# Cross attention over 64 head groups: the value products of two groups in one run, and value loads at another place in the queue

## The chip, the cores and the metric

The kernel runs on one core of one Trainium2 chip. The metric is the device time of one execution in microseconds. Engines: TensorE (PE, its weight loads PEld), VectorE (DVE), ScalarE (ACT), GpSimd (POOL), and SyncE (SP), which here only issues transfers (DMAs).

## The reference, cut to what matters

`x` and the context have shape (8, 256, 1024), all f32, and there are 32 heads of 32. Keys and values are both the context itself.

```python
xn = (x - mean(x)) * rsqrt(var(x) + 1e-5) * gamma + beta      # over the last axis
Q, K, V = split_heads(xn @ Wq.T), split_heads(ctx), split_heads(ctx)
scores = where(mask, einsum('bhsd,bhtd->bhst', Q, K) * 32 ** -0.5, -inf)
attn = einsum('bhst,bhtd->bhsd', softmax(scores), V)           # heads joined again
out = x + attn @ Wout.T
```

## The kernel before, in words

The attention is cut into 64 quads: quad n is batch n // 8 and the four heads of group n % 8. One iteration n of the main loop (a slot) holds, for every engine, what it does in that slot; each engine runs its instructions in the order in which the program writes them. In slot n:

- TensorE computes the scores of quad n + 1 (`scores`, L486: 32*128 tiles, four score banks), then the value products of quad n - 2 (`values`, L629: 64*32 tiles, 32 matmuls in the program, 64 in the trace), then full 128*128 work: query products for later quads (L345, L447) and output products for the batch before (`product_steps`, L715). Both projections are computed with seven products of halves in place of eight, from sums of halves which POOL makes (`sum_x`, `sum_at`, `sum_wq`, `sum_wo`). The table STEPS says how many output steps stand before the values, behind them and at the end of each slot.
- `softmax(n + 1)` spreads over DVE (maximum and mask, L522; reciprocal, L533; 32x32 transposes of probabilities into pT, L541), ACT (exponentials, L526; `aside`, L547, which copies half of pT to pc; `copy_at`, L642, which evicts finished value products from PSUM into the buffers at; `copy_q` and others) and POOL (normalization, L535). `copy_at` for all finished quads stands behind the exponentials of the first head.
- SP then moves blocks of probabilities between partitions: two transfers pT<-pT (L607), other loads of the slot (the list `between`: keys every second slot, residual rows, weights kept in DRAM, and x for a later batch), two transfers pT<-pc (L611). The second two wait for the first two to land. The load of the values of quad n (`load_v`, L144), which waits for quad n - 2's products to be done with the buffer, is issued in slot n ahead of the moves of quad n + 1 (list `ahead`). At the end of a slot follow moves of normalized x (`move_x`, L332, six of them in some slots), weights to keep (`keep_wq`), and stores of the output (L758).

Buffers: pT has three, v two, at three, the value products' PSUM pool `ps_v` two banks, the scores' pool four. So the products of quad n - 2 must be done before softmax(n + 1) can write pT, and a value load waits for the products two quads before.

`sum_at` makes the sums of the attention output. S1 = S2 + A11 is made on POOL at the end of the sixth slot of a block (i = 5), in the place of S2, and reads the first half buffer of at; i = (n - 8) % 8. Ahead of the main loop stand 32 transposes of the identity (`busy`, L120), which keep TensorE at work until x has been loaded and normalized.

Of the kernel before, what the change touches and what calls it, by code (L numbers as in the profile page):

```python
# [46 lines left out]
F32 = mybir.dt.float32  # L47
# [4 lines left out]
P = 128  # L52
# [7 lines left out]
def xattn_kernel(  # L60
# [12 lines left out]
    B, S, D = x.shape  # L73
# [3 lines left out]
    NQ = NC  # L77
    NH = P // HD
    NS = S // P
    NT = T // P  # L80
    NO = D // 512
    K = 32
# [4 lines left out]
    N = B * NQ  # L87
# [16 lines left out]
    ps_v = ctx.enter_context(tc.tile_pool(name="ps_v", bufs=2, space=PS))  # L104
# [11 lines left out]


    busy = ps_s.tile([P, P], F32, tag="sc", name="busy")
    for _ in range(32):
        nc.tensor.transpose(busy, ident, ident)  # L120


# [2 lines left out]
    def load_x(b, s, h=None):  # L125

        if b not in xs:
            xs[b] = xp.tile([P, NS, D], F32, tag="x", name=f"x_{b}")
        cols = ds(0, D) if h is None else ts(h, 512)
        nc.sync.dma_start(xs[b][:, s, cols], x[b, ts(s, P), cols])  # L130
# [9 lines left out]
    def load_v(n):  # L140

        b, g = divmod(n, NQ)
        vs[n] = vp.tile([P, NI, P], F32, tag="v", name=f"v_{n}")
        nc.sync.dma_start(  # L144
            vs[n],
            kv[b, g // 2, :, ds(2 * T + n % 2 * NI * P, NI * P)].rearrange("p (i v) -> p i v", i=NI),
        )
# [164 lines left out]
    def blocks_x(b, s):  # L312

        if s == 0:
            xes[b] = xp.tile([P, NA, NC, NS, K], F32, tag="x", name=f"xe_{b}")
        nc.vector.transpose(
            xes[b][:, :, :, s, :],
            xs[b][:, s, :].rearrange("p (c q k) -> p q c k", c=NC, q=NA),
        )

    def move_x(b, part):

        if 0 in part:
            tile_ = lnp.tile([P, NC * (S + 1)], F32, tag="xnT", name=f"xnT_{b}")
            xnT = tile_[:, : NC * S].rearrange(
                "p (a c s k) -> p a c s k", a=NA, c=NC, s=NS
            )
            to_move[b] = xnT
            xnTs[b] = lambda c: xnT[:, :, c, :, :]
        for i in part:  # L330
            a, q = i % NA, (i + i // NA) % NA
            nc.sync.dma_start(to_move[b][ts(q, K), a], xes[b][ts(a, K), q])  # L332
# [138 lines left out]
    mbs, scs, pTs, pvs, ats, pos = {}, {}, {}, {}, {}, {}  # L471
# [146 lines left out]
            tail()  # L618
        yield

    def values(n):
        pvs[n] = [
            ps_v.tile([P, 2, NS, K], F32, tag="pv", name=f"pv_{n}_{r}") for r in range(2)
        ]
        pT = pTs.pop(n)
        for i in range(NI):
            for j in range(NH):
                for r in range(2):
                    nc.tensor.matmul(  # L629
                        pvs[n][r][j * HD : (j + 1) * HD],  # L630
                        vs[n][ts(r, 2 * K), i, ts(j, HD)],
                        pT[ts(r, 2 * K), :, i, j, :, :],
                        start=(i == 0), stop=(i == NI - 1),
                    )
# [160 lines left out]
    for n in range(N):  # L795
# [12 lines left out]
    loads, stats, norms, trans, moves, biases, masks = (  # L808
        {n: [] for n in range(N)} for _ in range(7)
    )  # L810
    for b in range(1, B):
# [3 lines left out]
        elif b == 2:  # L815
            when = dict(
                loads=(0, 1), stats=(2, 3), norms=(3, 3), trans=(4, 5),
                moves=tuple(5 + (i + 2) // 6 for i in range(16)),
            )
        else:  # L820
            when = dict(
                loads=(first - 12, first - 11) if b == SPLIT else (first - 13, first - 12),
# [84 lines left out]
    for b in range(B - 1):  # L907
        done, ends = 0, b == B - 2
        for i, counts in enumerate(steps_of(b)):
            n = NQ * (b + 1) + i  # L910
# [10 lines left out]
    def project_steps(n, place):  # L921
        for one in steps.get((n, place), ()):
            product_steps(*one)


    for n in range(N):
        b, i = divmod(n - NQ, NQ)
        new_q = new_qs[n]
        between = []
        if n % 2 == 0 and n + 4 < N:  # L930
            between.append(partial(load_k, n + 4))
        ahead = [partial(load_v, n)] if n > 1 else []
        between += rings[n]
        if b >= 0:
            if b == B - 2 and i - 1 in (5, 6):
                between.append(partial(send, b, *ENDS_TO[i - 1]))
            if i < 4:
                between.append(partial(load_res, b, *((0, 0), (0, 1), (1, 1), (1, 0))[i]))
        between += [partial(load_x, *args) for args in loads[n]]
        between += [partial(load_mask, one) for one in masks[n]]  # L940
        if n in (3, 4):
            between.append(partial(load_wo, B21, n - 3))
        if n == N - 4:
            again = xp.tile([P, NS, D], F32, tag="x", name="x_again")
            for s in range(NS):
                between.append(partial(nc.sync.dma_start, again[:, s, :], x[B - 1, ts(s, P), :]))

        if n + 1 < N:
            scores(n + 1)
        project_steps(n, 0)  # L950
        hooks, now, behind = {}, [], []
        for what, one, *args in evacuations[n]:
            if one == B - 2:
                now.append(partial(what, one, *args))
            else:
                place = 0 if i in (3, 4, 6) or i < 3 and what is not add_p1 else "soon" if i == 2 else 1
                if one not in P1_ASIDE and i in (1, 2):
                    place = "p1" if what is keep_p1 else "soon"
                hooks.setdefault(place, []).append(partial(what, one, *args))
        if n >= 2:  # L960
            values(n - 2)
        project_steps(n, 1)
        copies = [partial(copy_q, q) for q in new_q]
        if n in halves and n % 2 == 0:
            make_q(halves[n], second=True, chunks=range(NC // 2, NC))
            copies.insert(0, partial(copy_q, halves[n]))
        for q in new_q:
            make_q(q)
        if n in products:
            query_product(*products[n])  # L970
            copies.append(partial(copy_product, *products[n]))
        for one in now:
            one()
        fill = []
        if n < 2:
            transpose_x1(2 * n)
            transpose_x1(2 * n + 1)
            fill = [partial(copy_x1, 2 * n), partial(copy_x1, 2 * n + 1)]
        elif n <= NQ:
            fill = [partial(ln_stats, *args, parts=(i,)) for args in stats[n] for i in range(3)]  # L980
            fill += [partial(blocks_x, *args) for args in trans[n]]
        if n + 1 < N:
            softmax(n + 1, copies, ahead, between, hooks, fill)
        else:
            copy_at(n - 2)
            for load in ahead + between:
                load()
        if b >= 0 and i == 1:
            sum_at(b, "S2", *((slice(NK - 1, NK),) if b == B - 2 else ()))
        later = []  # L990
        if n > NQ:
            for args in stats[n]:
                ln_stats(*args, later=later)
        for args in norms[n]:
            ln_norm(*args, nc.scalar)
        if n > NQ:
            for args in trans[n]:
                blocks_x(*args)
        for args in moves[n]:
            move_x(*args)  # L1000
        for one in away[n]:
            one()
        for one in biases[n]:
            mask_bias(one)
        project_steps(n, 2)
        for one, slot in S3_SLOTS:
            if n == slot:
                sum_at(one, "S3")
        if b >= 0:
            for name in {2: ("S4",), 3 if b == B - 2 else 5: ("S1",)}.get(i, ()):  # L1010
                sum_at(b, name)
            if i == 0 and b == B - 2:
                sum_at(b, "S2", slice(0, NK - 1))
        for slot, name in ((n + 2, "S1"), (n + 2, "S2"), (n + 1, "S4"), (n - 1, "S3")):
            if slot in firsts:
                sum_x(firsts[slot], name)
        if b == B - 2:
            if i > 2:
                add_kept(b, i, *ENDS_TO[i])
        elif b >= 0 and i in (3, 4, 5):  # L1020
            add_p1(b, *{3: (0, 1), 4: (1, 1), 5: (1, 0)}[i])
        for one in later:
            one()
        if n in halves and n % 2:
            make_q(halves[n], second=True, chunks=range(NC // 2))
        if n == 0:
            nc.gpsimd.tensor_scalar(gs, gam, NEG_SCALE, 1.0, ALU.mult, ALU.mult)
        if n < NQ:
            fold(n)
        for one in sums[n]:  # L1030
            one()
        if N - NQ + 2 < n < N - 1:

            c = n - (N - NQ + 3)
            if c == 0:
                last = ps_q.tile([P, 512], F32, tag="pq", name="po_last")
            end_steps(last, "A11", B11, (c,), (0,))
# [100 lines left out]
```

## Time and profile before

| | |
|---|---|
| three timed runs | 576.61, 577.20, 577.48 us; median 577.2 |
| the profiled execution, from its first to its last instruction | 577.0 us |
| TensorE / weight loads / VectorE / ScalarE / GpSimd busy | 567.3 / 394.2 / 460.4 / 411.7 / 409.8 us |
| share of transfer time, SP's queue | 66.8% of 16 engines' span |
| HBM read / written | 60.04 / 10.49 MB |

The profiled execution is another one than the timed ones; its own time is told by its span alone, and that lies within them. In rows of a timeline the first number is the start in microseconds from the first instruction, the second the time from the first start to the last end of a run of like instructions, then come engine, line, operation, output <- input, form, count, and in brackets how long the engine had been idle before and what ended that. A matmul in the program is two in the trace. Matmuls are pipelined, so a run's stretch overlaps the start of the next.

### The profile page before, as it was taken

To read this page: it belongs to the slowest core of one execution; us is meant where nothing else is said; L and a number is where in the kernel's file an instruction comes from. 1 tells how busy PE (TensorE), PEld (TensorE's weight loads), DVE (VectorE), ACT (ScalarE), POOL (GpSimd) and SP (SyncE) were. 2 spreads that over 40 slices of the span, in tenths; PEclk is the share of its full clock that TensorE was granted. 3 is DMA by queue.
4 is the path that set the end of the run, shared out by engine and by line. 5 is a ranking of instruction groups with operands and counts; after the bars stand their busy time and mean duration, and the time that the engine had idled before them with its cause. 6 is when DMAs were issued, how large, how long until landed. Compare 5 with 4: busy or idle time off the path is not lost. (4 is left out here: it accounts for less than half of the span.)

```text
span 577.0 us, 20128 instructions
## 1 busy us (share of the span) xinstructions
PE 567.3 (98%) x7162; PEld 394.2 (68%) x7162; DVE 460.4 (80%) x1695; ACT 411.7 (71%) x1425; POOL 409.8 (71%) x677
## 2 busy tenths in 40 slices
PE   8999998999999999999999999999999999999997
PEld 8788784667667777677676677667766767755543
DVE  5888887788877879979888788988878878779823
ACT  4697886677667877688677867768767776769810
POOL 1778898889896896876568675676658657448770
PEclk9999999899999999999999999999999999999999
DMA  8974766656677777957678856687567864446751
GB/s 304 394 206 126 208 161 180 192 148 166 185 220 222 200 208 207 271 166 201 188 213 228 211 138 189 212 240 206 148 161 236 224 170 130 130 138 178 199 166 73
DMA packets 50100, 111.69 MB, mean 194 GB/s; under 512 B 9424, under 2 KB 10192, under 8 KB 50000
## 3 DMA queue, kind: packets, MB, share of 16 engines
q1 hardware_dynamic: 49712, 110.40, 66.8%
q8 instruction: 57, 0.93, 0.7%
q14 instruction: 43, 0.35, 0.2%
q10 hardware_dynamic: 288, 0.01, 0.0%
HBM read 60.04 MB, written 10.49 MB: 122 GB/s over the span
## 5 line engine op out<-in xcount | busy, mean ns | idle before, releaser
L535 POOL TENSOR_SCALAR e<-e,rden 128x256 f32<-128x256 f32 x512 | 236.0, 478 | 116.9 <-DVE rden L533 114.4
L526 ACT ACTIVATE e<-e,mn 128x256 f32<-128x256 f32 x512 | 253.9, 501 | 50.7 <-DVE mn L522 49.6
L541 DVE STREAM_TRANSPOSE pT<-e 128x512 f32<-128x512 f32 x256 | 180.9, 707 | 44.7 <-POOL e L535 32.7
L522 DVE CUSTOM_DVE_ANT_0 e<-sc,mb 128x256 f32<-128x256 f32 x512 | 185.4, 416 | 26.4 <-PE sc L486 26.0
L547 ACT COPY pc<-pT 128x512 f32<-128x512 f32 x128 | 79.0, 617 | 72.1 <-DVE pT L541 36.6
L526 ACT ACTIVATION_READ_ACCUMULATOR e<-e,mn 128x1 f32 x512 | 97.9, 191 | 0.0
L345 PE MATMUL pq<-xnT,wq 128*128 128x256 f32 (+1 forms) x368 | 84.1, 383 | 0.6 <-ACT qa L354 0.6
L345 PEld LDWEIGHTS pq<-xnT,wq 128*128 128x128 f32 x368 | 68.9, 190 | 15.4 <-issue 3.7
L629 PE MATMUL pv<-pT,v 64*32 64x128 f32 x4096 | 74.7, 274 | 3.5 <-DMA v<-in_kv_dram 2.9
L629 PEld LDWEIGHTS pv<-pT,v 64*32 64x32 f32 x4096 | 57.5, 105 | 26.7 <-issue 14.7
L486 PEld LDWEIGHTS sc<-k,qa 32*128 32x128 f32 x1024 | 46.2, 184 | 41.9 <-issue 23.6
L715 PE MATMUL po_S<-wo,at 128*128 128x512 f32 x152 | 74.3, 606 | 0.0
L486 PE MATMUL sc<-k,qa 32*128 32x256 f32 x1024 | 73.6, 401 | 0.1
L715 PE MATMUL po_A<-wo,at 128*128 128x512 f32 x128 | 61.2, 620 | 0.3 <-ACT qa L354 0.3
L715 PE MATMUL po_S<-wo,s 128*128 128x512 f32 x104 | 49.9, 606 | 0.0
L533 DVE RECIPROCAL rden<-den 128x2 f32<-128x2 f32 x256 | 37.6, 147 | 7.7 <-ACT e L526 6.8
L522 DVE DVE_READ_ACCUMULATOR2_ANT mn<- 128x1 f32 x512 | 42.5, 83 | 0.0
L715 PEld LDWEIGHTS po_A<-wo,at 128*128 128x128 f32 x128 | 23.4, 193 | 26.2 <-issue 24.5
L447 PEld LDWEIGHTS pq_A<-xnT,wq 128*128 128x128 f32 x320 | 37.3, 192 | 4.8 <-issue 3.6
L715 PEld LDWEIGHTS po_S<-wo,at 128*128 128x128 f32 x152 | 25.8, 190 | 19.7 <-issue 19.1
L447 PE MATMUL pq_A<-xnT,wq 128*128 128x128 f32 x320 | 37.3, 275 | 0.0
L748 POOL TENSOR_TENSOR r<-r,p 128x512 f32<-128x512 f32 x23 | 29.4, 1278 | 7.1 <-DMA r<-in_x_dram 3.3
(96 smaller groups left out, 608.7 us busy)
## 6 DMA issues: line engine op xcount, KB each, us to landing
v<-in_kv_dram SPq DMA_DIRECT2D x64, 256.0 KB, 3.9
pT<-pT SPq DMA_DIRECT2D x128, 128.0 KB, 3.1
pT<-pc SPq DMA_DIRECT2D x128, 128.0 KB, 3.5
ring<-kept_T SPq DMA_DIRECT2D x18, 512.0 KB, 5.2
k<-in_kv_dram SPq DMA_DIRECT2D x32, 256.0 KB, 3.1
x<-in_x_dram SPq DMA_DIRECT2D x14, 512.0 KB, 5.1
r<-in_x_dram SPq DMA_DIRECT2D x28, 256.0 KB, 5.1
out_dram<-r SPq DMA_DIRECT2D x28, 256.0 KB, 3.0
```

The source lines that it names most:

```text
L345: nc.tensor.matmul(pqs[n], wq[:, o, c, :], xnTs[b](c), start=(c == 0), stop=(c == NC - 1),)
L447: nc.tensor.matmul(pqs[b][:, o, :], w[:, c], x_[:, c], start=begins and o + c == 0, stop=c == NK - 1, skip_group_check=True,)
L486: nc.tensor.matmul(scs[n][j][:, s, :], qa[r, n % NQ, ts(s, P)], ks[n - n % 2][r, n % 2, :], start=True, stop=True,)
L522: nc.vector.tensor_tensor_reduce(out=e[:, s, :], in0=pss[j][:, s, :], in1=mbs[n // NQ], scale=1.0, scalar=NO_SCORE, op0=ALU.add, op1=ALU.m ...
L526: nc.scalar.activation(e[:, s, :], e[:, s, :], AF.Exp, bias=mn[:, s : s + 1], scale=-1.0, accum_out=den[:, s : s + 1],)
L533: nc.vector.reciprocal(rden, dens[j])
L535: nc.gpsimd.tensor_scalar(es[j][:, s, :], es[j][:, s, :], rden[:, s : s + 1], 1.0, ALU.mult, ALU.mult,)
L541: nc.vector.transpose(pT[:, :, :, j, :, :].rearrange("p a i s k -> p (a i) s k"), es[j].rearrange("p s (b t) -> p b s t", t=K),)
L547: nc.scalar.copy(pc[:, :, ts(j, 2)], pT[:, 1, :, ts(j, 2)])
L629: nc.tensor.matmul(pvs[n][r][j * HD : (j + 1) * HD], vs[n][ts(r, 2 * K), i, ts(j, HD)], pT[ts(r, 2 * K), :, i, j, :, :], start=(i == 0), s ...
L715: nc.tensor.matmul(po, operand(b, name)[:, c], wo[:, which, c], start=begins and c == 0, stop=c == NK - 1, skip_group_check=not begins,)
L748: nc.gpsimd.tensor_tensor(r, r, p1s[b], ALU.add)
```

## The change

In 18 odd slots (PAIRS: 11, 13, 15, 19, 21, 23 and so on to 55, three in each block of eight) TensorE computes the value products of quads n - 2 and n - 1 one behind the other, into two PSUM tiles of twice the size; the even slot behind each has no value products. Quads of the other slots are done one at a time as before. The eviction of both quads then stands in the odd slot. Value loads of quads 8 to 56 are issued one slot sooner in the program's order: right behind the moves of probabilities, ahead of moves of x, kept weights and stores. From slot 6 on the loads of x no longer stand between the two kinds of moves of probabilities, but behind the moves of x at the end of the slot. S1 is made one slot sooner (i = 4). Of the 32 transposes ahead of the loop 29 are left. Pools and their numbers of buffers stay.

```diff
-    for _ in range(32):
+    for _ in range(29):
         nc.tensor.transpose(busy, ident, ident)
...
-    def values(n):
-        pvs[n] = [
+    def values_pair(n):
+        both = [
+            ps_v.tile([P, 2, 2, NS, K], F32, tag="pv", name=f"pv_{n}_{r}") for r in range(2)
+        ]
+        for i in range(2):
+            values(n + i, [tile_[:, i] for tile_ in both])
+
+    def values(n, to=None):
+        pvs[n] = to or [
             ps_v.tile([P, 2, NS, K], F32, tag="pv", name=f"pv_{n}_{r}") for r in range(2)
         ]
...
+    EARLY_V = range(NQ, N - NQ + 1)
+    PAIRS = [n for n in range(NQ + 3, N - NQ, 2) if n % NQ != 1]
+
     for n in range(N):
...
-        ahead = [partial(load_v, n)] if n > 1 else []
+        ahead = [partial(load_v, n)] if n > 1 and n not in EARLY_V else []
...
-        between += [partial(load_x, *args) for args in loads[n]]
+        if n < NQ - 2:
+            between += [partial(load_x, *args) for args in loads[n]]
...
-        if n >= 2:
+        if n in PAIRS:
+            values_pair(n - 2)
+        elif n >= 2 and n - 1 not in PAIRS:
             values(n - 2)
...
+        if n + 1 in EARLY_V:
+            load_v(n + 1)
         for args in moves[n]:
             move_x(*args)
+        if n >= NQ - 2:
+            for args in loads[n]:
+                load_x(*args)
...
-            for name in {2: ("S4",), 3 if b == B - 2 else 5: ("S1",)}.get(i, ()):
+            for name in {2: ("S4",), 3 if b == B - 2 else 4: ("S1",)}.get(i, ()):
                 sum_at(b, name)
```

## The prediction

> **What bounds the kernel now.** I read the page first, then TensorE's own waits, then TensorE's timeline stretch by stretch, and last SP's timeline around each place where TensorE waited.
>
> ```profile
> span 577.0 us, 20128 instructions
> PE 567.3 (98%) x7162; PEld 394.2 (68%) x7162; DVE 460.4 (80%) x1695; ACT 411.7 (71%) x1425; POOL 409.8 (71%) x677
> ```
> ```profile
> PE pv L629 <- DMA v<-in_kv_dram: 2.9, 2, 2.1
> ```
>
> TensorE is busy for 567.3 of 577.0 us, so a microsecond can be gained only by making its work denser or by taking away one of its few waits; the largest wait is for value loads, 2.9 us in two places. "Busy" hides how dense the work is. For that I take the starts of the runs in two slots in which the order of the runs differs (in slot 17 an output product stands between scores and values).
>
> ```profile
> 153.95 1.15 PE L486 MATMUL sc<-k,qa 32*128 32x256 f32 x16
> 155.02 1.16 PE L629 MATMUL pv<-pT,v 64*32 64x128 f32 x64
> 156.11 1.98 PE L715 MATMUL po_S<-wo,at 128*128 128x512 f32 x4
> ```
> ```profile
> 161.48 1.15 PE L486 MATMUL sc<-k,qa 32*128 32x256 f32 x16
> 162.55 3.70 PE L715 MATMUL po_A<-wo,at 128*128 128x512 f32 x8
> 166.18 1.16 PE L629 MATMUL pv<-pT,v 64*32 64x128 f32 x64
> 167.27 3.72 PE L345 MATMUL pq<-xnT,wq 128*128 128x256 f32 x16
> ```
> ```profile
> 368.91 1.15 PE L486 MATMUL sc<-k,qa 32*128 32x256 f32 x16
> 370.90 1.26 PE L629 MATMUL pv<-pT,v 64*32 64x128 f32 x64 [0.85 <-DMA v<-in_kv_dram]
> 372.09 6.28 PE L715 MATMUL po_A<-wo,at 128*128 128x512 f32 x14
> ```
>
> The output runs of 14 and of 8 differ by 6.28 - 3.70 = 2.58 us, so one 512-column matmul streams in 0.43 us, 0.84 ns a column. A value run is 64 matmuls of 128 columns in 64*32 tiles, eight of which fill the array: 1,024 columns one after another, 0.86 us. It takes 166.18 to 167.27 = 1.09 us, also 155.02 to 156.11 = 1.09. So each value run has about 0.23 us in which nothing streams, wherever it stands. A score run takes 1.07 us before values (153.95 to 155.02) and 1.07 before an output product (161.48 to 162.55): what follows it makes no difference.
>
> **Part 1: the pairs.** The list PAIRS names 18 odd slots (11, 13, 15, 19, ... 55): three in each block of eight from slot 8 to slot 55. In each, the value products of quads n-2 and n-1 are one run of 128 matmuls, and slot n+1 has none. The instructions are the same; one fixed part of 0.23 us goes per pair. The score run of the even slot is then followed by a 128*128 run, which the row at 162.55 shows at no extra price. Ends: 0, if the second set starts afresh as the first does, and 18 x 0.23 = 4.1 us. I take 4.1, since the second set keeps the tile form and the row of the first shows its 0.23 to lie outside the streaming. Nothing here can make the run longer than two runs.
>
> **Part 2: value loads sooner.** Each load of v from slot 8 on stands in SP's queue right behind the moves of probabilities of its slot, no longer behind moves of x, stores and kept weights. The v that slot 41 waited for:
>
> ```profile
> 361.65 5.03 SPq L332 DMA_DIRECT2D xnT<-xe  x6
> 366.77 0.53 SPq L758 DMA_DIRECT2D out_dram<-r  x1
> 367.39 0.41 SPq L144 DMA_DIRECT2D v<-in_kv_dram  x1
> ```
>
> It moves to about 361.65, 5.7 us sooner. The wait in slot 41 was 370.90 - 368.91 - 1.07 = 0.92 us, with 0.10 us in the value row (1.26 against 1.16): 1.0 us goes. The probabilities of that quad were sent before 361.65, so nothing else is late there. The six moves and the store now follow the load; the moves are used two slots on, the store by nobody.
>
> **Part 3: slots 9 to 11.** Here TensorE lost more:
>
> ```profile
> 91.11 1.26 PE L629 MATMUL pv<-pT,v 64*32 64x128 f32 x64 [0.55 <-DMA pT<-pT]
> 97.98 1.15 PE L486 MATMUL sc<-k,qa 32*128 32x256 f32 x16
> 101.18 1.25 PE L629 MATMUL pv<-pT,v 64*32 64x128 f32 x64 [2.05 <-DMA v<-in_kv_dram]
> 102.36 3.68 PE L715 MATMUL po_A<-wo,at 128*128 128x512 f32 x4
> 110.50 1.16 PE L629 MATMUL pv<-pT,v 64*32 64x128 f32 x64
> ```
> ```profile
> 102.36:105.86 3.50, 3.50 (x10) 1.44 (x5) 2.87 (x18) 3.01 (x13) 3.37 (x4) 0.52 0.82 222
> ```
> ```profile
> 93.96 3.75 SPq L332 DMA_DIRECT2D xnT<-xe  x6
> 97.81 0.53 SPq L144 DMA_DIRECT2D v<-in_kv_dram  x1
> ```
> ```profile
> 107.22 1.15 SPq L611 DMA_DIRECT2D pT<-pc  x2
> ```
> ```profile
> 109.08 0.41 SPq L144 DMA_DIRECT2D v<-in_kv_dram  x1
> ```
>
> Slot 9 waited 0.55 us for probabilities, slot 10 waited 101.18 - 97.98 - 1.07 = 2.13 us for its values, and then the granted clock was 0.52 for 3.5 us (third number from the end of the stretch's row): four output matmuls took 3.68 us where 156.11 shows 1.98, another 1.70. Together 4.4 us. The load issued at 97.81 now goes ahead of the six moves, 3.75 us sooner, so slot 10's wait goes. But slot 11 is the first pair and needs quad 10 a slot sooner. Its probabilities are sent at 107.22 and its v at 109.08; without the x loads and the store ahead of it perhaps at 107, landing at 110 to 111. Without the losses TensorE reaches that second set at 110.50 + 0.86 - 4.4 = 107.0. It waits there 3 to 4 us instead, and may fall to the lower clock once more. So nearly all of it is given back: I take 0.5 us gained, with 4.4 gained and 2.0 lost as the ends.
>
> The Trainium skill ("TensorE: Matmul & The Clock Gate", section on HAM oscillation) says that TensorE must have no idle gap of over about 3.4 us if the clock is to stay up. The row at 101.18 speaks for less: a wait of 2.05 us was followed by the low clock, while 0.85 us at 370.90 was not. By the page slot 10 should have lost 1.7 us less; the measurement decides.
>
> **Part 4: what the pairs have to wait for.** In the other 17 pairs quad n-1 has two slots, not three, from scores to values. Block 6 shows the room:
>
> ```profile
> 453.71 0.53 SPq L758 DMA_DIRECT2D out_dram<-r  x1
> 454.34 0.40 SPq L144 DMA_DIRECT2D v<-in_kv_dram  x1
> ```
> ```profile
> DMA to landing us min/median/max: 3.4/3.4/3.4
> ```
> ```profile
> 467.78 0.52 SPq L144 DMA_DIRECT2D v<-in_kv_dram  x1
> ```
> ```profile
> DMA to landing us min/median/max: 6.2/6.2/6.2
> ```
> ```profile
> 455.81 1.16 PE L629 MATMUL pv<-pT,v 64*32 64x128 f32 x64
> ```
> ```profile
> 473.69 1.16 PE L629 MATMUL pv<-pT,v 64*32 64x128 f32 x64
> ```
> ```profile
> v<-in_kv_dram SPq DMA_DIRECT2D x64, 256.0 KB, 3.9
> ```
>
> Quad 50 (used second in slot 51): its v goes ahead of the store, to 453.71, lands 3.4 us later at 457.1; the second set is due at 455.81 + 0.86 = 456.7. It waits 0.4 us. Quad 52 (slot 53): its scores begin a pair slot, whose query product ends 0.86 us later, and ScalarE's copy of queries stands in front of its copy of probabilities, so I shift its load by 0.86 to 468.64; with 6.2 us it lands at 474.84, due at 473.69 + 0.86 - 0.2 = 474.35: 0.5 us. With the median of 3.9 us it would land 1.8 us early. So a block waits between 0 and 0.9 us; the third pair of a block (quads 22, 30, ...) loses the x load that stood between its moves and has room. Half of 0.9 over the five blocks from slot 17 is 2.2 us, my value; the ends are 0 and, with 0.4 us more in the two tight pairs of each, 6.
>
> **The rest.** Three of 32 warm-up transposes go.
>
> ```profile
> 6.52 1.23 PE L120 MATMUL busy<-ring 128*128 128x128 f32 x8
> ```
> ```profile
> 6.10 0.81 DVE L257 TENSOR_SCALAR x<-x,mv,rstd 128x1024 f32<-128x1024 f32 x1
> ```
>
> Eight take 1.23 us, 0.15 each: 0.46 us for three. Their successor needs x, normalized at 6.91, so TensorE can start sooner; but it waits again at slot 9 for transfers, which absorbs that. I take 0.1, ends 0 and 0.6. ScalarE evicts four values in an odd slot and none in the even one, all four behind the pair's last product: this delays exponentials of the same quads by up to 0.8 us, in the same stretch in which the 0.86 above holds them anyway, so I count it once. The sum S1 moves up a slot on POOL, since the pair's second eviction writes the buffer that S1 reads:
>
> ```profile
> 471.86 1.27 POOL L748 TENSOR_TENSOR r<-r,p 128x512 f32<-128x512 f32 x1
> ```
>
> In slot 52 it would run at 471.86, 1.3 us long, and be done 2 us ahead of the eviction behind 473.69 + 1.6; the addition shown here then runs behind it. Cost: nothing, as long as those 2 us cover it; up to 1 us a block if they did not. The x loads behind the moves start some 7 us later and are used two slots on: nothing, except in slot 9, which the ends of part 3 hold.
>
> **Sum.** 577.0 - 4.1 - 1.0 - 0.5 - 0.1 + 2.2 = 573.5 us for the profiled execution; the median of the runs is 577.2, 0.2 above its span, so I forecast 573.7.
>
> **Rivals.** (a) *Faster than that*: slots 9 to 11 keep their whole gain and no pair waits: 4.1 + 1.0 + 4.4 + 0.1 = 9.6 below 577.2, 567.6 us. For it: SP has idle time between those moves once the x loads are gone; against it: the row at 107.22. Chance 0.16. (b) *Slower*: the second sets become the bound. From scores to values the chain through VectorE, ScalarE, POOL and two moves has 2 slots; where the late v of slot 53 (6.2 us) is the rule, twelve pairs wait about 0.8 us instead of the 0.2 that I count on average, 7 us more, slot 11 loses 2 instead of gaining 0.5: 573.7 + 7.2 + 2.5 = 583; with half of it 578.5. It decides from a mean wait of (4.1 + 1.6) / 18 = 0.32 us a pair. For it: two of three pairs in block 6 have no room; against it: the median landing. Chance 0.18. (c) *No gain from pairing*: the second set pays its 0.23 us again, or the waits just equal the gain: 573.7 + 3.5 = 577.2. Chance 0.12.
>
> **How the numbers follow.** The forecast's own case (570 to 576) has 0.54, (a) 0.16, (b) 0.18, (c) 0.12. About 0.2% (1.2 us) is what a measurement can tell from no change. Faster by more: 0.54 + 0.16 = 0.70; same 0.12; slower 0.18. The range leaves out half of (a) and the worse half of (b): 568.5 to 578.5.
>
> **What would show it.** Right: value runs of 128 matmuls at about 1.95 us; no wait for v in slots 10 and 41; waits of 0 to 1 us inside pair runs on pT or v, one of 3 to 4 us in slot 11. Wrong: paired runs of 2.2 us; waits above 1 us in most pairs; TensorE waiting for evictions or DVE on scores; a granted clock below 1 in several places.

## The result and the profile after

| | before | changed |
|---|---|---|
| timed runs, median (lowest to highest) | 577.2 us (576.61 to 578.73, 5 runs) | 602.69 us (595.83 to 603.64, 5 runs) |
| ratio, 95% interval | | 1.0405 (1.0358 to 1.0453) |
| profiled execution, span | 577.0 us | 597.7 us |

The change is 4% slower; the forecast was 573.7 us with a range of 568.5 to 578.5. The page of the changed kernel, span and busy times:

```profile
span 597.7 us, 20116 instructions
PE 571.4 (96%) x7159; PEld 395.6 (66%) x7159; DVE 459.2 (77%) x1695; ACT 414.4 (69%) x1425; POOL 411.3 (69%) x677
```

Every engine has the work it had, and the span is 20.7 us longer. TensorE's busy time grew by 4.1 us (571.4 against 567.3), in part at a lower clock, as shown below; the other 16.6 us are waiting. I cut the span into slots, from the first score product of one slot to that of the next, and took the differences to the kernel before:

| where | longer by, us |
|---|---|
| slots 9 to 12 (slot 10: -3.9; slot 11, the first pair: +9.0) | +4.9 |
| slots 26, 34 and 42, which are not pairs | +2.5, +4.3, +3.1 |
| the 17 other pairs with the even slots behind them | +7.9 |
| slot 41 | -1.0 |
| slots 0 to 8, warm-up included | -0.8 |

The third and the fifth line are less certain: a single pair can differ by over 1 us between two profiles of one kernel (slot 55 by 1.4 us between e10 and e15 below), slots 0 to 8 by some tenths. The cause of the second line, as shown below, is the place of the x loads, which the prediction put at nothing. The first place is the one the prediction argued about. TensorE's timeline of the changed kernel (start, length of the run, engine, line, form, count, idle time before), then SP's, VectorE's, and last the busy times and, third number from the end, the granted clock of one stretch:

```profile
99.16 1.16 PE L636 MATMUL pv<-pT,v 64*32 64x128 f32 x64
...
105.61 3.23 PE L486 MATMUL sc<-k,qa 32*128 32x256 f32 x16
109.38 1.25 PE L636 MATMUL pv<-pT,v 64*32 64x128 f32 x64 [0.54 <-DMA pT<-pT]
113.92 1.56 PE L636 MATMUL pv<-pT,v 64*32 64x128 f32 x64 [3.29 <-issue]
115.41 5.04 PE L722 MATMUL po_S<-wo,s 128*128 128x512 f32 x8
```
```profile
98.05 0.58 SPq L130 DMA_DIRECT2D x<-in_x_dram  x1
...
109.58 1.15 SPq L611 DMA_DIRECT2D pT<-pc  x2
110.82 0.53 SPq L144 DMA_DIRECT2D v<-in_kv_dram  x1
```
```profile
103.13 1.29 DVE L231 BATCH_NORM_STATS2 st<-x 128x6 f32<-128x512 f32 x2 [4.53 <-DMA x<-in_x_dram]
```
```profile
113.90:117.40 3.50, 3.48 (x67) 2.08 (x68) 2.62 (x16) 3.50 (x13) 2.32 (x4) 0.62 0.37 85
```

Slot 10 (99.16) no longer waits for its values. Slot 11 loses at three points. Its scores take 3.23 us and not 1.15: an x load, now issued at 98.05, reaches VectorE so late that it idles 4.53 us before the statistics of that x, and the masks of the scores before, which stand behind these on VectorE, free the score banks late. The second set waits 3.29 us, because its values are asked for only at 110.82 and land 3.0 us later. Then the clock falls to 0.62 over the next 3.5 us: eight output matmuls take 5.04 us where 3.70 was usual.

The second place, slot 26. TensorE, SP, and the waits of the changed kernel that belong to it (engine, line, waited for: us in total, times, longest):

```profile
253.77 2.05 PE L447 MATMUL pq_S<-sx,ring 128*128 128x128 f32 x16 [1.02 <-DMA ring<-kept_T]
256.79 1.98 PE L722 MATMUL po_S<-wo,s 128*128 128x512 f32 x4 [0.97 <-DVE r L764]
```
```profile
236.41 0.58 SPq L130 DMA_DIRECT2D x<-in_x_dram  x1
...
237.87 1.15 SPq L607 DMA_DIRECT2D pT<-pT  x2
239.06 0.59 SPq L414 DMA_DIRECT2D ring<-kept_T  x1
242.98 1.56 SPq L611 DMA_DIRECT2D pT<-pc  x2
...
247.56 0.43 SPq L414 DMA_DIRECT2D ring<-kept_T  x1
248.04 0.43 SPq L151 DMA_DIRECT2D r<-in_x_dram  x1
```
```profile
POOL r L755 <- DMA r<-in_x_dram: 14.7, 4, 5.8
DVE r L764 <- POOL r L755: 13.3, 4, 4.9
```

And SP in the same two slots of the kernel before:

```profile
221.87 0.60 SPq L130 DMA_DIRECT2D x<-in_x_dram  x1
...
229.72 1.15 SPq L607 DMA_DIRECT2D pT<-pT  x2
230.91 0.58 SPq L414 DMA_DIRECT2D ring<-kept_T  x1
232.62 1.14 SPq L611 DMA_DIRECT2D pT<-pc  x2
...
237.41 0.45 SPq L414 DMA_DIRECT2D ring<-kept_T  x1
```

SP does not issue L611 until the transfers of L607 have landed. Before, an x load of 512 KB was issued at 221.87, eight us ahead of the first moves at 229.72, and SP stood between them and L611 from 231.5 to 232.62. In the changed kernel x is issued at 236.41, 1.5 us ahead of the moves at 237.87, and SP stands from 239.65 to 242.98. Everything behind it in the queue is late by that: the second half of the weight ring (247.56, for which TensorE waits until 253.77) and a residual row (248.04), for which POOL waits, then VectorE, then TensorE. So a wait of SP that hurt nobody became a wait of TensorE. Slots 34 and 42 have the same order on SP.

### The profile page after: what moved, and what is told of

The parts are those of the page before. It is cut to its first block, busy times and chain, and to the rows that moved or that the text cites. A ratio compares the mean times of both kernels' runs of the same rounds, so it can differ in the third digit from the quotient of the medians.

```text
span 597.7 us, 20116 instructions
## 1 busy us (share of the span) xinstructions
PE 571.4 (96%) x7159; PEld 395.6 (66%) x7159; DVE 459.2 (77%) x1695; ACT 414.4 (69%) x1425; POOL 411.3 (69%) x677
## 5 line engine op out<-in xcount | busy, mean ns | idle before, releaser
L526 ACT ACTIVATION_READ_ACCUMULATOR e<-e,mn 128x1 f32 x512 | 100.1, 195 | 0.0
L636 PEld LDWEIGHTS pv<-pT,v 64*32 64x32 f32 x4096 | 59.3, 105 | 31.2 <-issue 20.9
L486 PE MATMUL sc<-k,qa 32*128 32x256 f32 x1024 | 76.3, 403 | 0.1
L722 PE MATMUL po_A<-wo,at 128*128 128x512 f32 x128 | 59.5, 605 | 0.0
L722 PE MATMUL po_S<-wo,s 128*128 128x512 f32 x104 | 52.2, 627 | 3.5 <-DVE r L764 3.4
```

Source lines behind the costliest of these rows:

```text
L486: nc.tensor.matmul(scs[n][j][:, s, :], qa[r, n % NQ, ts(s, P)], ks[n - n % 2][r, n % 2, :], start=True, stop=True,)
L526: nc.scalar.activation(e[:, s, :], e[:, s, :], AF.Exp, bias=mn[:, s : s + 1], scale=-1.0, accum_out=den[:, s : s + 1],)
L636: nc.tensor.matmul(pvs[n][r][j * HD : (j + 1) * HD], vs[n][ts(r, 2 * K), i, ts(j, HD)], pT[ts(r, 2 * K), :, i, j, :, :], start=(i == 0), s ...
L722: nc.tensor.matmul(po, operand(b, name)[:, c], wo[:, which, c], start=begins and c == 0, stop=c == NK - 1, skip_group_check=not begins,)
```

## The experiments

All are read as ratios to the kernel before, measured beside them on the same chip (its medians there were 575.6 to 576.9 us). The runs stand on several chips, so I take differences between them from the ratios; 1% is 5.8 us.

| | edit | us, median | ratio (95%) |
|---|---|---|---|
| e1_no_pairs | the change without pairs | 586.66 | 1.0198 (1.0160 to 1.0236) |
| e2_x_back | the change, x loads where they were | 584.24 | 1.0128 (1.0086 to 1.0170) |
| e3_v_early | the kernel before, value loads sooner | 574.32 | 0.9971 (0.9955 to 0.9987) |
| e4_same_quad | the change, second sets need nothing new | 586.71 | 1.0181 (1.0137 to 1.0224) |
| e5_no_first_pair | e2 without the pair in slot 11 | 579.25 | 1.0064 (1.0036 to 1.0092) |
| e6_same_x_back | e4 with the x loads of e2 | 574.92 | 0.9973 (0.9943 to 1.0004) |
| e7_x_ahead | e1, x loads ahead of the moves of x | 573.20 | 0.9952 (0.9934 to 0.9969) |
| e8_pairs_3 | e2 with five pairs | 575.95 | 0.9989 (0.9968 to 1.0010) |
| e9_v_ahead | e2, second value loads sooner still | 582.00 | 1.0111 (1.0080 to 1.0143) |
| e11_x_ahead_pairs | the change, x loads as in e7 | 582.56 | 1.0110 (1.0091 to 1.0130) |
| e10_both | e9 and e11, without the pair in slot 11 | 578.09 | 1.0038 (1.0016 to 1.0060) |
| e13_pages_x_back | e2, instruction count shifted | 583.33 | 1.0121 (1.0081 to 1.0161) |
| e12_pages | e10, count shifted by a whole packet | 580.62 | 1.0078 (1.0052 to 1.0105) |
| e14_half_page | e10, count shifted by half a packet | 575.25 | 0.9973 (0.9949 to 0.9997) |
| e15_both_again | e10, beside e14 | 579.27 | 1.0040 (1.0020 to 1.0061) |

The times of e2, e6, e8, e12 and, by less than a microsecond, e1, e7 and e15 lie outside every range that I had given them; e9 and e10 came out in the rival's range.

**The three parts apart.** My theory was that there are three causes with prices of their own: x loads at a place where SP waits behind them, pairs whose second sets wait, and value loads, which gain. The rival was that all of the loss is the pairs'.

```diff
 e1: the change
-    PAIRS = [n for n in range(NQ + 3, N - NQ, 2) if n % NQ != 1]
+    PAIRS = []
 e2: the change
-        if n < NQ - 2:
-            between += [partial(load_x, *args) for args in loads[n]]
+        between += [partial(load_x, *args) for args in loads[n]]
...
-        if n >= NQ - 2:
-            for args in loads[n]:
-                load_x(*args)
 e3: the kernel before
-        ahead = [partial(load_v, n)] if n > 1 else []
+        ahead = [partial(load_v, n)] if n > 1 and n not in EARLY_V else []
...
+        if n + 1 in EARLY_V:
+            load_v(n + 1)
         for args in moves[n]:
 e4: the change; the second quad's products take pT and v of the first
-            values(n + i, [tile_[:, i] for tile_ in both])
+            values(n + i, [tile_[:, i] for tile_ in both], n)
```

e1_no_pairs. 

> The changed kernel with the list PAIRS empty: one value run in every slot as before; early value loads, x loads behind the moves, S1 a slot sooner and 29 transposes stay. Theory 1 (three separate causes: waits of the second set in pair slots, some 14 us with slot 11; the x loads behind the moves, which delay ring weights and residual rows in slots 26, 34 and 42, some 10 us; early value loads, 1 to 5 us gained): the late ring stays, so 580 to 586 us. Rival (all of it comes from the pairs, which hold up ScalarE and SP's queue and so the ring too): 571 to 576 us, no wait for the ring.

e2_x_back. 

> The changed kernel with the x loads between the two kinds of moves of probabilities again; pairs and early value loads stay. Theory 1 (the x loads' new place costs the 10 us in slots 26, 34, 42): 590 to 594 us, no wait for ring weights in those slots. Rival (pairs cause the late ring): 600 to 605 us with the waits still there.

e3_v_early. 

> The kernel before with the value loads alone issued a slot sooner, behind the moves of probabilities. If slots 9, 10 and 41 were waits for late value loads only: 572 to 576 us (1.0 us in slot 41, up to 4.4 in slots 9 and 10). If what was ahead of the load (moves of x, stores, kept weights) now comes too late: 577 to 580.

e4_same_quad. 

> The changed kernel, but the second set of each pair multiplies the probabilities and values of the first quad again, so that it has the same matmuls and nothing to wait for; the value products of 18 quads are left out. If the second sets' waits are what the pairs cost (8.9 us in slots 19 to 55 and about 5 in slots 9 to 12): 586 to 591 us, and pair runs of 2.0 us throughout. If the 128-matmul run or the eviction of both quads is what costs: 598 to 603 us.

The rival fell with e1: without any pair the kernel is still 2% slower. Value loads alone gain 0.3%. Against e3, the x loads' new place costs 1.0198 - 0.9971 = 2.27%, 13.1 us, without pairs, and pairs cost 1.0128 - 0.9971 = 1.57%, 9.1 us, without it. Both together with e3's gain make a ratio of 1.0355, where the change has 1.0405 (1.0358 to 1.0453); with intervals of about 0.4% on e1 and e2 too, a loss by the two together is not shown. e4 stands beside e1 (1.0181 and 1.0198): with the x loads behind the moves, pairs that wait for nothing new cost nothing that can be measured. e2 came out 6 us below what I had expected, in part because I had counted the x loads in three slots only: once they are put back, the 17 later pairs cost 4.5 us in the profile and not 7.9. SP's wait for the first moves, in the kernel before and then in e1:

```profile
SPq L611 <- DMA pT<-pT: 75.9, 59, 6.2
```
```profile
SPq L611 <- DMA pT<-pT: 94.3, 59, 7.0
```

**The place of the x loads.** In e7 the same loads stand in the same slot, but ahead of the six moves of x and not behind them.

```diff
+        if n >= NQ - 2:
+            for args in loads[n]:
+                load_x(*args)
         for args in moves[n]:
             move_x(*args)
-        if n >= NQ - 2:
-            for args in loads[n]:
-                load_x(*args)
```

e7_x_ahead. 

> No pairs, early value loads, and the x loads ahead of the moves of normalized x rather than behind them: the same volume in the same slot, but issued several us before the next slot's first moves of probabilities. Theory (an x load is dear only when it stands right ahead of those first moves, for whose landing SP waits before it issues anything else): SP's wait for them falls from about 94 us in all to below 60, slots 26, 34 and 42 lose their 2 to 6 us each, and the time falls from 586.7 to 574 to 577. Rival 1 (any x load outside the stretch between the two sets of moves delays them, by its volume): 583 to 588. Rival 2 (the x itself comes too late for VectorE): 586 stays, and VectorE is seen waiting for x.

SP's waits in e7, and its timeline in the slots shown above:

```profile
SPq L611 <- DMA pT<-pT: 64.3, 54, 7.4
```
```profile
221.49 0.43 SPq L130 DMA_DIRECT2D x<-in_x_dram  x1
...
227.38 1.14 SPq L607 DMA_DIRECT2D pT<-pT  x2
228.56 0.58 SPq L414 DMA_DIRECT2D ring<-kept_T  x1
229.97 1.15 SPq L611 DMA_DIRECT2D pT<-pc  x2
...
234.75 0.43 SPq L414 DMA_DIRECT2D ring<-kept_T  x1
```

x now has 5.9 us before the first moves follow, and SP stands from 229.14 to 229.97. The ratio is 2.46% below e1's, 14.2 us, and the lowest of all kernels here, 0.5% below the kernel before. (The wait of L611 came out at 64.3 us in all, not below the 60 that I gave; slots 34 and 42 are free of losses, slot 26 keeps 0.9 us.) It is the place that costs, not the volume. e11 makes the same move in the whole change:

e11_x_ahead_pairs. 

> The whole change with one edit: the x loads stand ahead of the moves of normalized x, not behind them. Theory (an x load costs by standing right ahead of the next slot's first moves of probabilities, and the pairs, which have less room, pay for the same lateness once more): the time falls from 602.7 to about 583, which is 573.2 for the x loads in that place without pairs and some 10 us for the pairs. Rival (pairs lose what x loads cost wherever those stand): 590 or more.

582.56 for 583: the x loads' place was 1.0405 - 1.0110 = 2.95% of the change, 17.0 us, against the 14.2 without pairs. The intervals are too wide to show that the two differ. In the profiles the 17 later pairs cost 4.9 us here and 7.9 in the change, so some of the pairs' waits came from the x loads. I take the reason to be that the loads held up behind SP's wait then include values that a second set needs at once; no run isolates it.

**What pairs cost.** e5 leaves out the first pair, e6 takes the waits for data from all pairs, e8 keeps five, e9 moves the second quad's value load ahead of that quad's own moves of probabilities:

```diff
 e5, e8: e2 with
+    PAIRS = [n for n in range(NQ + 5, N - NQ, 2) if n % NQ != 1]     # e5
+    PAIRS = [n for n in range(2 * NQ + 3, N - NQ, NQ)]               # e8
 e9: e2 with
         ahead = [partial(load_v, n)] if n > 1 and n not in EARLY_V else []
+        if n % 2 and n + 1 in EARLY_V:
+            ahead.append(partial(load_v, n + 1))
...
-        if n + 1 in EARLY_V:
+        if n + 1 in EARLY_V and n % 2 == 0:
             load_v(n + 1)
```

e5_no_first_pair. 

> The change with the x loads back between the moves of probabilities, and without its first pair (slot 11 and slot 12 run their own values; 17 pairs are left). Theory (the first pair alone is dear, because its second set waits over 3 us and the granted clock then drops): slots 11 and 12 fall from 25.9 to about 20.3 us, the slowest wait inside a pair is about 2 us, and the time falls from 584.2 to about 578. Rival (all pairs cost alike, about 0.5 us each): it falls by 0.5 us only, to about 583.7.

e6_same_x_back. 

> The change with the x loads back between the moves, and with the second set of each pair reading the probabilities and values of the pair's first quad, so that it has nothing to wait for; the products of the 18 second quads are left out. What pairing itself saves is then all that stands between this kernel and the one with early value loads alone (574.3 us). Theory (a pair saves 0.05 to 0.15 us, since part of the fixed time of a run comes back in the neighbouring runs): 571.5 to 573.5 us. The prediction's term (0.23 us a pair): 570.2 us. Rival (pairs cost something even without a wait, through the evictions that stand behind the whole run): 576 or more.

e8_pairs_3. 

> Early value loads, x loads between the moves as before, and only five pairs, one in each block from slot 16 on, in the slots (19, 27, 35, 43, 51) whose pairs had the most room. Theory: no wait but 0.6 us in slot 43, and 5 x 0.14 us saved: 573.5 to 574.5 us, no different from early loads alone (574.3) to within what can be measured, faster than the kernel before by 0.2 to 0.4%. Rival (pairs cost 0.5 us each wherever they stand): 576.8.

e9_v_ahead. 

> The change with the x loads between the moves (584.2 us before) and, as its one other edit, the value load of each pair's second quad issued a little sooner still: ahead of that quad's own moves of probabilities, where SP would otherwise wait for the first of them to land. Theory (the second sets wait for v, because its load stands in SP's queue behind that wait; where landings can be read, v lands last, as 315.63 + 3.2 = 318.83 against a second set that starts at 318.89): the waits inside the pairs of slots 13 to 55 go, slot 11 waits about 1 us less (until its second moves land) and keeps its low clock or part of it, and the time falls to 577 to 580. Rival (the second moves of probabilities land as late as v): 582 to 585.

The first pair alone costs 1.0128 - 1.0064 = 0.64%, 3.7 us, with intervals of 0.4 and 0.3%; in the profiles slots 11 and 12 together are 5.6 us shorter without it. That is some half of the 9.1 us that pairs cost. e6 stands where e3 stands (0.9973 against 0.9971): with no data to wait for, 18 pairs gain nothing that can be measured, where 0.23 us each would be 0.7% (its interval is 0.3%). A clean pair does gain a little. Slots 27 and 28 of e2, then of e3 (the view ends inside the last row, hence 12 matmuls and not 16):

```profile
254.31 1.15 PE L486 MATMUL sc<-k,qa 32*128 32x256 f32 x16
255.39 2.11 PE L636 MATMUL pv<-pT,v 64*32 64x128 f32 x128
257.43 1.98 PE L722 MATMUL po_S<-wo,s 128*128 128x512 f32 x4
...
272.05 1.15 PE L486 MATMUL sc<-k,qa 32*128 32x256 f32 x16
```
```profile
246.98 1.15 PE L486 MATMUL sc<-k,qa 32*128 32x256 f32 x16
248.06 1.16 PE L629 MATMUL pv<-pT,v 64*32 64x128 f32 x64
249.15 1.98 PE L715 MATMUL po_S<-wo,s 128*128 128x512 f32 x4
...
264.86 0.93 PE L486 MATMUL sc<-k,qa 32*128 32x256 f32 x12
```

The run of 128 takes 2.04 us (255.39 to 257.43), two runs of 64 take 2 x 1.09; over the two slots it is 17.74 against 17.88. That is 0.14 us for the best third of the pairs; for slots 23 and 24 the sum over both is 0.02 us longer than in e3. e8 shows no gain either, and lay 1.5 us above my number. e9 came out where the rival had it, and its ratio is no different from e2's (1.0111 and 1.0128): the waits of slots 29 and 53 went (0.15 and 1.1 us), slot 35 waited 0.8 us more, and those of slots 21 and 55 stayed. What these two waited for was not data. In e2:

```profile
207.22 0.27 PE L636 MATMUL pv<-pT,v 64*32 64x128 f32 x1 [0.86 <-issue]
...
499.55 0.41 PE L636 MATMUL pv<-pT,v 64*32 64x128 f32 x4 [1.66 <-issue]
```

The last matmul of slot 21's pair and the last four of slot 55's wait, in the middle of a set that had been running on the same data. "issue" is a wait for nothing that the profile shows; slot 11 carries the same mark, but there the wait stands between the sets, and ends when values land.

**Both repairs.** e10 puts e9's and e11's edits together, without the pair in slot 11.

e10_both. 

> The change with both repairs and without its first pair: x loads ahead of the moves of normalized x, the value load of each second quad ahead of that quad's moves of probabilities, pairs in slots 13 to 55. Theory: no wait is left inside pairs, and a pair saves about 0.05 us: 571.5 to 574 us, no slower than the x loads in that place without pairs (573.2) and faster than the kernel before by 0.4 to 0.8%. Rival (the pairs keep waits of their own through ScalarE's evictions): 577 or more.

A miss: 578.09. With both repairs the pairs still cost 0.9% against e7.

**Waits for instructions.** Instructions come over a queue of their own. The page of e2 counts 57 packets and 0.93 MB on one such queue, 16 KB each; e12 below, with 256 more instructions for TensorE, has 58:

```profile
q8 instruction: 57, 0.93, 0.7%
```
```profile
q8 instruction: 58, 0.95, 0.7%
```

e2's trace has 14,549 records of TensorE (7,159 matmuls, as many weight loads, 231 others), 255 for each of its 57 packets. So I take this queue to be TensorE's, and a packet to be 256 instructions.

I looked up the packet before each wait that stands within a set, and counted TensorE's records up to the matmul that waits:

| kernel, slot | packet ends | TensorE goes on | after | place in the list, modulo 256 |
|---|---|---|---|---|
| changed, 21 | 207.82 | 209.11 | 1.29 | 193 |
| changed, 55 | 511.87 | 513.33 | 1.45 | 194 |
| e2, 21 | 205.85 | 207.22 | 1.37 | 193 |
| e2, 55 | 498.16 | 499.55 | 1.39 | 194 |
| e9, 21 and 55 | 204.28, 495.94 | 205.64, 497.23 | 1.36, 1.29 | 193, 193 |
| e6, 13 and 31 | 126.79, 284.81 | 128.17, 286.16 | 1.38, 1.35 | 194, 193 |

The place is the same one within a packet each time. So it is in all profiles: those of kernels with pairs, e14's aside, have 21 waits inside a set that nothing in the profile ended, of 0.4 to 1.75 us, and all stand at 193 or 194. From the start of the packet before it to the matmul that goes on are 2.3 to 2.9 us each time (204.66 to 207.22 in slot 21 of e2). A pair is 128 matmuls with 128 weight loads, a whole packet used up in the 2.04 us above. The kernels without pairs have no such wait (before, e1, e3, e7). e13 and e12 shift the list, by issuing early query projections in 128-column products (the edit as in e13):

```diff
+    HALVED = range(NQ, 2 * NQ)
...
     def make_q(n, second=False, chunks=range(NC)):
...
-        for c in chunks:
-            nc.tensor.matmul(
-                pqs[n], wq[:, o, c, :], xnTs[b](c), start=(c == 0), stop=(c == NC - 1),
-            )
+        whole = n not in HALVED or len(chunks) < NC
+        for half in (slice(0, None),) if whole else (ts(0, P), ts(1, P)):
+            for c in chunks:
+                nc.tensor.matmul(
+                    pqs[n][:, half], wq[:, o, c, :], xnTs[b](c)[:, half],
+                    start=(c == 0), stop=(c == NC - 1),
+                )
```

e13_pages_x_back. 

> The change with x loads between the moves (584.2 us), with five early query projections (slots before 16) issued as 128-column instead of 256-column products: the same streaming time, 40 matmuls and 40 weight loads more, so that TensorE's instruction count stands 80 higher from there on. Theory (the unexplained waits are waits for TensorE's own instructions, which come in packets of 16 KB: every such wait seen so far stands at position 193 or 194 modulo 256 in TensorE's list of instructions and ends 1.25 to 1.65 us after the end of such a packet): the waits before the last matmuls of slots 21 and 55 (0.86 and 1.66 us) and the one behind slot 43 (0.45) go, and any new one stands where a boundary now falls within some 20 instructions of a pair's end, which the count gives as slots 15, 35 or 47, again at 193 or 194 modulo 256; the time hardly moves, 582 to 585. Rival (they are waits for data): slots 21 and 55 keep their waits of 0.9 and 1.7 us at the same matmuls.

e12_pages. 

> Both repairs without the first pair (578.1 us), with eight query projections issued as 128-column products, so that TensorE's instruction count stands 128 higher behind slot 16. By the count the boundaries of 16 KB then fall near the end of a pair in slots 37 and 39 alone, and no longer in 21, 43 and 55. Theory (waits for instructions are what keeps the pairs from any gain): 574 to 576 us, with at most one wait of that kind. Rival (the pairs wait for probabilities, in other slots from run to run): 577 to 579.

I had counted the products as written; each is two matmuls and two weight loads in the trace, so e13's shift was 160 and not 80, and e12's was 256, a whole packet, which changes nothing. In e2 place 193 lies 106 and 116 records ahead of the ends of the pairs in slots 27 and 39; plus 160, less 256, that is 10 and 20. e13's timeline:

```profile
256.23 0.41 PE L641 MATMUL pv<-pT,v 64*32 64x128 f32 x5 [1.07 <-issue]
```
```profile
362.73 0.43 PE L641 MATMUL pv<-pT,v 64*32 64x128 f32 x10 [1.73 <-issue]
```

They are the pairs of slots 27 and 39, with 5 matmuls left (10 instructions) and with 10 left (20), at places 193 and 194 again, 1.57 and 1.50 us after their packets. Slots 21 and 55 have no wait any more. The slots that I had named were wrong with the wrong shift; by the right one, worked out after the run, the waits follow the list, and e14 below tests that ahead of its run. e12 kept slot 21's wait at place 193, and was no better than e10 (1.0078 against 1.0038), so the smaller products by themselves gain nothing. So I shifted by half a packet, with the same kernel unshifted beside it:

e14_half_page. 

> Both repairs without the first pair, with four early query projections in 128-column products. Each written product is two matmuls and two weight loads in the trace (7159 became 7239 with five projections, 7287 with eight), so eight projections had shifted TensorE's list by 256, a whole packet, that is by nothing, and five by 160; four shift it by 128, half a packet. By that count no pair but slot 37's (21 instructions ahead of its end) has a boundary near its end. Theory: the waits at position 193 in slots 21 and 55 are gone, at most slot 37 shows one, and the time is 1 to 3 us below that of the same kernel without the shift, run beside it. Rival (the rest is waits for data): the two are alike within 0.2%.

e15_both_again. 

> The same kernel without the shift, for comparison on one chip: 577 to 579 us as measured before (578.1), with a wait at position 193 in slot 21 in the profile.

575.25 against 579.27 us: 4.0 us, by the ratios 0.67% with intervals of 0.2% on each, where I had given 1 to 3. The two kernels differ in the place of the packet boundaries and in four projections of smaller products. The same two pairs, slots 13 and 55, in e15 and then in e14:

```profile
128.05 0.45 PE L636 MATMUL pv<-pT,v 64*32 64x128 f32 x14 [1.17 <-issue]
...
495.49 0.42 PE L636 MATMUL pv<-pT,v 64*32 64x128 f32 x6 [1.08 <-issue]
```
```profile
125.23 2.25 PE L641 MATMUL pv<-pT,v 64*32 64x128 f32 x128
...
491.59 2.10 PE L641 MATMUL pv<-pT,v 64*32 64x128 f32 x128
```

e15's profile has three such waits (slots 13, 21, 55), 2.8 us in all; e14's has none. The rest of the 4.0 us is within the intervals. Place 193 near the end of a pair makes such a wait possible and not certain: e10 is e15's kernel, and its profile has one, of 0.98 us in slot 21. Waits for the second moves of probabilities remain in both, in slots 27, 43 and 51 of e14 and 35, 43 and 51 of e15; whether these could be mended too was not tried. So even e14 is no faster than e7 (0.9973 and 0.9952): no kernel here shows a gain from pairs in its time.

The Trainium skill ("Runtime: NRT & Kernel Launch", section on instruction fetch mechanics) says that instructions come in blocks of 16 KiB over a queue of the engine's own, and that the cost of crossing from one block to the next is mostly hidden. The first half agrees with the 57 packets of 0.93 MB. The second holds for most packets here, and fails where a pair uses up a packet in 2.04 us: there waits of 0.4 to 1.75 us stand, one to three in each profile with pairs but e14's.

## Why the prediction was wrong

It was wrong in sign. Point by point, by its own steps:

- **The x loads** (*The rest*: "nothing, except in slot 9") are the step that failed most. I asked when x is used and not what stands behind it in the queue: SP's wait for pT<-pT to land, and on VectorE the masks behind the statistics. It cost 13 to 14 us without the pairs (e1 against e3 and e7), 17.0 with them (the change against e11). The kernel before showed that wait in SP's waits, 75.9 us in 59 places, and I had not asked who pays when it grows.
- **Part 3** had the mechanism, wait and lower clock in slot 11 both, and the wrong sum. The wait was 3.3 us, as said (3 to 4), and slot 10 gave its 3.9 back (its load went ahead of 3.85 us of moves by the rows, not 3.75). But slot 11 pays 9.0: 3.4 for the wait, 1.9 for the lower clock (1.3 in the output run, 0.5 in the second set), which I had named and not added, 0.95 for the second set itself, which slot 12 gives back, and 2.7 for scores and a first set that come late, as the x loads' place made them. The last is not the heart of it: with the x loads put back (e2) slot 11 still pays 7.7, since the wait is 3.6 and the lower clock lasts 6.8 us. Slot 9 lost 0.9 where it was to give 0.5; why stays open. Together 4.9 lost for 0.5 gained, beyond the worse end (2.0). e3 shows that the gain in slot 10 belongs to the value loads and needs no pair: its slot 10 is 3.9 us shorter too.
- **Part 1** (4.1 us, ends 0 to 4.1): the second set does not keep the 0.23 out of its way; a clean pair saves 0.14 at most, and 18 without waits for data save nothing measurable (e6 against e3), where two waits for instructions took 2.3 us. The lower end was right, by two effects of which I had one: part of the fixed time is paid again, and the pair's end waits for instructions.
- **Part 4** (2.2 us lost, ends 0 to 6): the 17 pairs after the first cost 7.9 us in the changed kernel's slots, what they save included. With the x loads put back they cost 1.0064 - 0.9971 = 0.93%, 5.4 us (e5 against e3), some of it waits for instructions, which no term had. Part 1's "Nothing here can make the run longer than two runs" was therefore wrong.
- **Part 2** was right: slot 41 lost its 1.0 us, and value loads alone gain 0.3% (e3), 1.7 us. By the two profiles slots 9, 10 and 41 give 5.7 us; single profiles show more here than the times.
- **Transposes, evictions, S1:** slots 0 to 8 are 0.8 us shorter, within what they differ by between runs; nothing in the slots shows a price of S1's place.

Rival (b) said "second sets the bound" and 578.5 to 583. The change falls there once the x loads are out of the way (582.56), but not by twelve late pairs: in e11's profile slots 11 and 12 cost 5.8 us and the 17 other pairs 4.9, of which waits for instructions are 1.7. That the number agrees is in part luck. Of the signs that I named, the run of 128 took 2.04 us, between right (1.95) and wrong (2.2), and waits of over 1 us stood in a few pairs only: no sign covered the x loads, the largest single cause.

## What to carry to other kernels

A load's price in a queue is set by what waits behind it, not by when its own data are used: look for instructions of that queue that wait for an earlier transfer, and keep large loads away from the front of that transfer. When an edit makes one engine's instructions denser, count them against the packets in which they arrive; waits without a releaser that sat at one place modulo 256 were waits for instructions here, and a shift of the list told them from waits for data. And sum a gain only once: what one part of a change gives without the other is not there to pay for the other.

## What the hardware showed that I had not expected

- TensorE can wait for its own instructions: 0.4 to 1.75 us, always at one place in a packet of 256, and it goes on 1.2 to 1.6 us after the end of the packet. The kernel with the list shifted by 128 instructions was 4.0 us faster (575.25 against 579.27).
- Waits of 2.05 us (slot 10 before) and of 3.29 us (slot 11 after) were each followed by 3.5 us at a mean granted clock of 0.52 and 0.62. But the changed kernel also waited 2.72 us in slot 34, for the weight ring, and 1.81 us in slot 9, and the granted clock stayed at 1.00: the length of a wait alone did not decide.
- A 512 KB load 1.5 us ahead of a transfer that SP waits for made that wait 3.3 us; 5.9 us ahead of it, 0.8 us.
